# State-space stage of a decoder: silu written with tanh, layernorm taken on tokens, x loaded first, residual added by TensorE

## The chip, the cores and the metric

One core of a Trainium2 chip runs the whole program. The metric is device time in microseconds (us), from the start to the end of one execution. The engines work side by side and meet through semaphores: TensorE (PE; its weight loads are shown as PEld), VectorE (DVE), ScalarE (ACT), GpSimd (POOL) and SyncE (SP), which here only issues transfers. ScalarE can issue transfers too.

## The reference, cut to what matters

Eight sequences of 256 tokens with 128 channels, in fp32, pass through three parts. The first is a state-space layer, which holds most of the change:

```python
Xn = (X - mu) * lax.rsqrt(var + 1e-05) * ln_g + ln_b
x  = silu(causal_depthwise_conv(Xn @ W_up1.T, K=4) + conv_b)      # 256 channels
pp = x @ W_ll.T + b_ll                   # 256 delta, 16 B, 16 C
delta = softplus(pp[..., :256]);  A = -exp(A_log)
A_bar = exp(delta * A)                   # 256 x 16 for each token
U = x * (A_bar - 1) / (delta * A) * delta * B
H_t = A_bar_t * H_{t-1} + U_t;    y_t = sum_n C_t[n] * H_t[:, n]
out = X + (y * silu(Xn @ W_up2.T)) @ W_down.T + b_down
```

Its caller adds X once more and takes a layernorm, so that the kernel computes 2X plus the projection. The second part is cross-attention, 16 heads of 64 channels, against a context of the same shape; the queries' input and the context each have a layernorm ahead of their projections. The third part is six layers of windowed attention and feed-forward, which the change does not touch.

## The kernel before, in words

The work is cut into four pairs of sequences (NPAIR), each 512 tokens wide (TP). Tiles hold channels on the 128 partitions and the tokens of a pair along the free axis, so that x and the context, which lie in memory by tokens, are transposed by TensorE after loading (t_ps, lines 319 and 161). A layernorm (layernorm_steps, lines 104 to 148) therefore sums over partitions: TensorE multiplies by a matrix of 1/128 for the mean (ln_mu, L108) and for the variance of the centred squares (ln_var, L120), and the root of the variance is Ln followed by Exp on ScalarE (inv_root, reported at L92).

For one pair, pre(p) makes everything that the scan needs. It loads and transposes x, normalises it into xn, and runs the convolution as 2 halves x 4 taps of matmuls on shifted views of xn (conv, L329), with the tap weights multiplied into the projection's ahead of time (w_tap, L290). Silu gives xm (L340). From xm TensorE forms B and C (bc_ps, L345), which ScalarE writes to DRAM through its own queue (L353), and delta (d_ps, L358), of which softplus is made as max(d, 0) (z, L367) plus ln(1 + exp(-|d|)) (ez, L365 and L92). The sum is dt (L371). The gate is a second silu (L392).

scan(p) runs 16 states n by 2 halves h. For each: rows n of B and of C come back from DRAM, broadcast over all partitions (rows, L455, SP's queue, 4 buffers); VectorE forms wz from xm, rows and 1/A (L460); GpSimd takes the difference of neighbours in time (dw, L465); ScalarE takes the exp of dt times A (ab, into two PSUM buffers, reported at L92); VectorE runs the recurrence, one instruction for each sequence (m, L444); GpSimd multiplies by C (mc, L446, 6 buffers); TensorE adds mc into the sum y by a multiplication with the identity (L424). From n = 2 on, wz reads a copy of xm in PSUM (xm_ps, L432). post(p) multiplies y by the gate (yg, L403), projects it (dn_ps, L408), adds the bias (L411) and 2x (r, L412) and takes the layernorm.

While pair p is scanned, steps of post(p-1) and of pre(p+1) are taken between the states; during the last two scans they are steps of project(0), which prepares cross-attention for the first pair (layernorms of context and latents, q, k and v). project(1) to project(3) run in the cross-attention loop, whose rounds consist of scores (s_ps, L993), values (o_ps, L1012) and sums (L1018) on TensorE. Each engine runs its own instructions in a fixed order, settled when the program is built. ScalarE's functions come from tables that have to be loaded: silu has a table of its own, while exp and ln are in one that load_table (L96) brings back. behind_exps and issue_after place an instruction behind the exps that are already in the order:

```python
            for h in range(2):
                m = sp.tile([P, TP], FP, tag=f"xm{h}", name="xm")
                with behind_exps():
                    A.activation(m, acc[h], AF.Silu, bias=col("conv_b", h))
                xm.append(m)
            load_table()
```

## Time and profile before

| what | value |
|---|---|
| time, median of 3 runs | 2323.32 us (2321.04 to 2324.24) |
| the profiled execution | 2323.17 us |
| its span in the profile | 2321.2 us |
| mean granted TensorE clock | 0.974 |
| busy share: PE, DVE, ACT, POOL | 93%, 77%, 64%, 71% |
| instructions: PE, DVE, ACT, POOL | 20240, 2486, 2483, 1437 |
| GpSimd's product with C (L446) | 128 instructions of 1277 ns on average |
| transfers of rows (L455) | 128 of 256 KB, 3.9 us from issue to landing |
| transfers of x | 4 of 256 KB, 5.4 us from issue to landing |

The profile page cuts the span into 40 slices of 58 us and gives the busy share of each engine there in tenths. In a line of the timeline the first number is the start in us, the second the length, then come engine, line of the program, operation, output and inputs with their shapes; "x3" means three instructions in a row, and the brackets at the end hold the idle time of the engine ahead of the instruction and what ended it. A line of the waits gives engine, tile and line, what was waited for, and then the total in us, the number of waits and the longest.

### The profile page before, as it was taken

How to read it: one execution, taken by the hardware profiler on the slowest of the kernel's cores; microseconds unless marked ns; L12 is line 12 of the kernel's file. 1: busy time of each engine (PE TensorE's matmuls, PEld its weight loads, DVE VectorE, ACT ScalarE, POOL GpSimd, SP SyncE). 2: the span in 40 equal slices, each digit the busy share in tenths (PEclk: the TensorE clock that was granted, in tenths of full speed). 3: DMA queues.
4: the chain of work that ended last, by engine and by line, in shares of the span. 5: the costliest groups of instructions: out<-in, count | busy, mean ns of one | idle time of the engine just before them, and what ended most of it. 6: DMA issues, size and time to landing. Idle time of an engine off the chain costs nothing.

```text
span 2321.2 us, 52828 instructions
## 1 busy us (share of the span) xinstructions
PE 2166.6 (93%) x20240; PEld 1347.3 (58%) x20240; DVE 1784.3 (77%) x2486; ACT 1483.5 (64%) x2483; POOL 1645.1 (71%) x1437
## 2 busy tenths in 40 slices
PE   7876888999998999999999999999999999999986
PEld 3232333444445666666666666666666766666664
DVE  4788886454457888888888888888888888888873
ACT  4434454455556766777777677677766776777664
POOL 3888886232368887777787777777777777777760
PEclk9887899999999999999999999999999999999999
DMA  4343331000203334343343334333343434333331
GB/s 128 96 114 93 98 98 41 1 6 1 80 18 60 65 63 88 65 74 61 71 80 69 71 63 80 71 71 67 62 85 71 73 60 78 62 61 62 57 66 32
DMA packets 438517, 154.38 MB, mean 67 GB/s; under 512 B 401918, under 2 KB 418172, under 8 KB 438140
## 3 DMA queue, kind: packets, MB, share of 16 engines
q1 hardware_dynamic: 438076, 150.75, 32.8%
q8 instruction: 163, 2.67, 0.5%
q14 instruction: 86, 0.70, 0.1%
q10 hardware_dynamic: 192, 0.26, 0.0%
HBM read 55.20 MB, written 1.31 MB: 24 GB/s over the span
## 4 chain that ended last, share of the span: by engine, by line
PE 34%; DVE 21%; ACT 20%; POOL 10%; issue 6%; DMA 0%; SPq 0%; POOLq 0%; ACTq 0%; DVEq 0%
DVE rb L617 4%; DVE qk L616 4%; PE qk_ps L599 4%; ACT sq L622 4%; ACT kz L668 3%; POOL pw L717 3%; PE f_ps L836 3%; POOL qk L620 3%; ACT pw L92 3%; PE qkT_ps L655 3%; PE o_ps L750 2%; DVE ss L629 2%; PE y_ps L769 2%; PE v_ps L599 2%; PE pr L214 2%
## 5 line engine op out<-in xcount | busy, mean ns | idle before, releaser
L620 POOL TENSOR_TENSOR qk<-qk,rb 128x512 f32<-128x512 f32 x384 | 484.5, 1283 | 108.4 <-DVE rb L617 88.8
L648 POOL TENSOR_TENSOR qk<-qk,rn 128x1024 f32<-128x1024 f32 x192 | 366.3, 1908 | 133.7 <-ACT rn L92 108.0
L599 PE MATMUL qk_ps<-wqkv,xs 128*128 128x512 f32 x768 | 364.9, 598 | 2.0 <-ACT sq L622 2.0
L622 ACT ACTIVATE sq<-qk_ps 128x1024 f32<-128x1024 f32 x192 | 196.8, 1025 | 179.0 <-DVE rb L617 169.2
L616 DVE TENSOR_TENSOR qk<-qk_ps,tab 128x1024 f32<-128x1024 f32 x192 | 233.3, 1215 | 79.7 <-PE qk_ps L599 78.8
L717 POOL TENSOR_TENSOR pw<-pw,mx 128x512 f32<-128x512 f32 x192 | 200.3, 1043 | 92.1 <-DVE mx L716 87.2
L629 DVE TENSOR_REDUCE ss<-sq 128x16 f32<-128x1024 f32 x192 | 232.5, 1211 | 40.3 <-ACT sq L622 37.5
L617 DVE TENSOR_TENSOR rb<-qk_ps,tab 128x1024 f32<-128x1024 f32 x192 | 233.2, 1214 | 0.0
L655 PE MATMUL qkT_ps<-ident,qk 128*128 128x128 f32 x1536 | 209.1, 279 | 15.1 <-ACT v L642 9.9
L92 ACT ACTIVATE pw<-pw 128x512 f32<-128x512 f32 x192 | 120.5, 628 | 155.0 <-POOL pw L717 154.7
L668 ACT COPY kz<-qkT_ps 64x1024 f32<-64x1024 f32 x192 | 193.1, 1006 | 34.8 <-PE qkT_ps L655 33.2
L750 PE MATMUL o_ps<-vz,pT 128*32 128x128 f32 x6144 | 207.5, 276 | 8.2 <-ACT pT L742 8.2
L731 POOL TENSOR_TENSOR pw<-pw,mx 128x512 f32<-128x512 f32 x192 | 200.3, 1044 | 19.5 <-DVE mx L730 17.9
L769 PEld LDWEIGHTS y_ps<-oT,wo 128*128 128x128 f32 x1536 | 186.3, 192 | 44.6 <-issue 36.8
L729 DVE TENSOR_REDUCE mx<-pw 128x8 f32<-128x512 f32 x192 | 130.5, 680 | 105.5 <-ACT pw L92 104.9
L1002 POOL TENSOR_TENSOR ws<-w 128x512 f32<-128x512 f32 x64 | 81.4, 1273 | 181.4 <-ACT w L92 171.5
L750 PEld LDWEIGHTS o_ps<-vz,pT 128*32 128x32 f32 x6144 | 156.0, 110 | 91.7 <-ACT rn L92 36.4
L703 PE MATMUL s_ps<-kz,qT 128*32 128x128 f32 x6144 | 203.0, 273 | 0.0
L599 PE MATMUL v_ps<-wqkv,xs 128*128 128x512 f32 x384 | 185.5, 606 | 16.6 <-ACT kz L668 16.5
L655 PEld LDWEIGHTS qkT_ps<-ident,qk 128*128 128x128 f32 x1536 | 164.9, 141 | 55.2 <-issue 43.6
L446 POOL TENSOR_TENSOR mc<-m,rows 128x512 f32<-128x512 f32 x128 | 163.3, 1277 | 40.8 <-issue 12.8
L599 PEld LDWEIGHTS qk_ps<-wqkv,xs 128*128 128x128 f32 x768 | 131.6, 191 | 96.5 <-issue 92.2
(180 smaller groups left out, 4237.5 us busy)
## 6 DMA issues: line engine op xcount, KB each, us to landing
vz<-v SPq DMA_DIRECT2D x1152, 64.0 KB, 2.1
rows<-bc_dram SPq DMA_DIRECT2D x128, 256.0 KB, 3.9
vz<-v SPq DMA_DIRECT2D x576, 32.0 KB, 2.0
wqkv<-in_L_ffn_Wqkv SPq DMA_DIRECT2D x18, 512.0 KB, 4.2
wo<-in_L_ffn_Wo SPq DMA_DIRECT2D x48, 64.0 KB, 2.0
w<-in_L_ffn_W SPq DMA_DIRECT2D x6, 341.0 KB, 3.3
t_in<-in_x SPq DMA_DIRECT2D x4, 256.0 KB, 5.4
wkv<-in_L_xattn_Wkv SPq DMA_DIRECT2D x1, 1024.0 KB
```

The costliest lines, as they stand in the source:

```text
L599: T.matmul(pr[:, i * 512 : (i + 1) * 512], lhsT=got[n]["xs"][:, tb * P : (tb + 1) * P], rhs=thirds[seq[n][0], c][:, i * 512 : (i + 1) * 51 ...
L616: V.tensor_tensor(t, p3, cs, ALU.mult)
L617: V.tensor_tensor(rb, p3, sn, ALU.mult)
L620: G.tensor_tensor(t[:, :, o], t[:, :, o], rb[:, :, f], ALU.add)
L622: A.activation(sq, p3, AF.Square)
L629: V.tensor_reduce(got[n]["ss"][:, 2 * c + tb, :], got[n]["sq"], AX.X, ALU.add)
L648: G.tensor_tensor(t, t, r, ALU.mult)
L655: T.transpose(t_ps[:, hb * P : (hb + 1) * P], t[:, 2 * hb : 2 * hb + 2, :].rearrange("p h d -> p (h d)"), ident,)
L668: A.copy(fixed3["kzs"][0][r, :, e, W + tb * P : W + (tb + 1) * P], t3[r])
L717: G.tensor_tensor(pw, pw, mx[:, 0].unsqueeze(3).to_broadcast(shape), ALU.subtract)
L750: T.matmul(o_ps[i * W : (i + 1) * W, j * P : (j + 1) * P], lhsT=pT[:, j, i * W : (i + 1) * W], rhs=vz[:, j, i].rearrange("p e d -> p (e d) ...
L769: T.matmul(y_ps[:, :P], lhsT=wts[d][0][:, hb, :], rhs=got[n]["oT", wh][:, hb, :], start=(hb == 0), stop=(hb == NHB - 1),)
```

## The change

Silu is computed as half its argument times (1 + tanh of half its argument). The halves are folded into the weights (w_tap, w_up2, half_b); tanh is taken from the table set that also holds exp, then 1 is added on ScalarE (for xm) or inside the product (for the gate), and VectorE multiplies. The number of table loads stays. The load that brings ln back stands behind the write of B and C. x of each pair and the context of each pair are normalised while tokens are on the partitions: bn_stats and bn_aggr on VectorE give mean and variance, and subtraction and scaling are four instructions (on ScalarE for x of pairs 1 to 3, on VectorE otherwise); only the result is transposed, and scale and shift are applied on the way out of PSUM. x itself is transposed as well, for the residual. The first load is that of x; identity and columns come over ScalarE's queue. The tap weights are formed after the first steps of pre(0), and the last steps of pre(0), the gate among them, are taken during scan 0. For pair 0 the rows of B of states 0 and 1 are broadcast by TensorE out of bc. The maximum z moves to ScalarE for pairs 1 to 3. 2x is added by a third matmul into the projection.

```diff
@@ -68,10 +68,12 @@
     def ps_o(name):
         return banks[-1].tile([P, 512], FP, tag="o", name=name)
 
+    t_in0 = keep.tile([P, 4, D], FP, name="t_in0")
+    nc.sync.dma_start(out=t_in0, in_=a["x"][0:2].rearrange("b (c q) d -> q (b c) d", q=P))
     ident = keep.tile([P, P], FP, name="ident")
-    nc.sync.dma_start(out=ident, in_=a["c_ident"])
+    nc.scalar.dma_start(out=ident, in_=a["c_ident"])
     cols = keep.tile([P, NCOL], FP, name="cols")
-    nc.sync.dma_start(out=cols, in_=a["cols"])
+    nc.scalar.dma_start(out=cols, in_=a["cols"])
     mean_w = keep.tile([P, P], FP, name="mean_w")
     G.memset(mean_w, 1.0 / D)
     eps_t = keep.tile([P, 1], FP, name="eps_t")
@@ -91,10 +93,8 @@
         with tc.issue_after(table[-1].ins) if table else ExitStack():
             return f(*args, **kw)
 
-    def load_table():
-        table.append(
-            tc.keep_in_program_order(A.preload_act_table_set("natural_log_exp_and_others"))
-        )
+    def load_table(name="natural_log_exp_and_others"):
+        table.append(tc.keep_in_program_order(A.preload_act_table_set(name)))
 
     def inv_root(dst, src, bias=0.0):
 
@@ -151,15 +151,33 @@
         for _ in layernorm_steps(*args):
             pass
 
-    def load_transposed(src, p, dst, pool):
-        t_in = pool.tile([P, 4, D], FP, name="t_in")
-        nc.sync.dma_start(
-            out=t_in, in_=src[2 * p : 2 * p + 2].rearrange("b (c q) d -> q (b c) d", q=P)
-        )
+    def turned_tokens(t):
         tp = ps_s("t_ps")
         for j in range(4):
-            T.transpose(tp[:, j * P : (j + 1) * P], t_in[:, j, :], ident)
-        A.copy(dst, tp)
+            T.transpose(tp[:, j * P : (j + 1) * P], t[:, j, :], ident)
+        return tp
+
+    def layernorm_tokens(t, on_act=False):
+
+
+        st = lnp.tile([P, 4, 6], FP, name="bn_st")
+        mv = lnp.tile([P, 4, 2], FP, name="bn_mv")
+        for j in range(4):
+            V.bn_stats(st[:, j, :], t[:, j, :])
+            V.bn_aggr(mv[:, j, :], st[:, j, :])
+        rs = lnp.tile([P, 4], FP, name="ln_rs")
+        inv_root(rs, mv[:, :, 1], eps_t)
+        if on_act:
+            V.scalar_tensor_tensor(mv[:, :, 0], mv[:, :, 0], -1.0, rs, ALU.mult, ALU.mult)
+        for j in range(4):
+            if on_act:
+                A.activation(
+                    t[:, j, :], t[:, j, :], AF.Identity, bias=mv[:, j, 0:1], scale=rs[:, j : j + 1]
+                )
+            else:
+                V.tensor_scalar(
+                    t[:, j, :], t[:, j, :], mv[:, j, 0:1], rs[:, j : j + 1], ALU.subtract, ALU.mult
+                )
 
     def one_by_one(*gens):
         for g in gens:
@@ -189,11 +207,16 @@
 
         wq, wkv = w2["wq"], w2["wkv"]
         sp = pools2[0]
-        ct = sp.tile([P, TP], FP, name="ct")
-        load_transposed(a["ctx_1024"], p, ct, sp)
+        t_in = sp.tile([P, 4, D], FP, name="t_in")
+        nc.sync.dma_start(
+            out=t_in,
+            in_=a["ctx_1024"][2 * p : 2 * p + 2].rearrange("b (c q) d -> q (b c) d", q=P),
+        )
+        yield
+        layernorm_tokens(t_in)
         yield
         cn = sp.tile([P, TP], FP, name="cn")
-        yield from layernorm_steps(ct, cn, col("ctx_w"), col("ctx_b"), fine=not p)
+        A.activation(cn, turned_tokens(t_in), AF.Identity, bias=col("ctx_b"), scale=col("ctx_w"))
         yield
         la = sp.tile([P, TP], FP, name="la")
         yield from layernorm_steps(x1[p], la, col("lat_w"), col("lat_b"), fine=not p)
@@ -252,7 +275,6 @@
             )
             return t_in
 
-        t_in = load_x(0)
         w_up1 = wp.tile([P, DI], FP, name="w_up1")
         nc.sync.dma_start(out=w_up1, in_=a["w_up1T"])
 
@@ -279,18 +301,28 @@
 
 
         w_tap = wp.tile([P, 2, KC, P], FP, name="w_tap")
-        for h in range(2):
-            r_ps = ps_s("tap_ps")
-            for k in range(KC):
-                T.matmul(
-                    r_ps[:, k * P : (k + 1) * P],
-                    lhsT=col("conv_w", h * KC + k).to_broadcast([P, P]), rhs=ident,
-                    start=True, stop=True,
-                )
-            V.tensor_tensor(
-                w_tap[:, h], r_ps.rearrange("p (k c) -> p k c", k=KC),
-                w_up1[:, h * P : (h + 1) * P].unsqueeze(1).to_broadcast([P, KC, P]), ALU.mult,
-            )
+
+        def taps():
+            for h in range(2):
+                r_ps = ps_s("tap_ps")
+                for k in range(KC):
+                    T.matmul(
+                        r_ps[:, k * P : (k + 1) * P],
+                        lhsT=col("conv_w", h * KC + k).to_broadcast([P, P]), rhs=ident,
+                        start=True, stop=True,
+                    )
+                V.scalar_tensor_tensor(
+                    w_tap[:, h], r_ps.rearrange("p (k c) -> p k c", k=KC), 0.5,
+                    w_up1[:, h * P : (h + 1) * P].unsqueeze(1).to_broadcast([P, KC, P]),
+                    ALU.mult, ALU.mult,
+                )
+
+
+        half_b = wp.tile([P, 2], FP, name="half_b")
+        V.tensor_scalar(half_b, cols[:, _OFF["conv_b"] : _OFF["conv_b"] + 2], 0.5, None, ALU.mult)
+        V.tensor_scalar(w_up2, w_up2, 0.5, None, ALU.mult)
+        twice = wp.tile([P, P], FP, name="twice")
+        V.tensor_scalar(twice, ident, 2.0, None, ALU.mult)
 
         xns = [wp.tile([P, 2, KC - 1 + S], FP, name=f"xn{i}") for i in range(2)]
         for t in xns:
@@ -314,13 +346,15 @@
             x = new_x(p)
             t_in = t_in or load_x(p)
             yield
-            tp = ps_s("t_ps")
-            for j in range(4):
-                T.transpose(tp[:, j * P : (j + 1) * P], t_in[:, j, :], ident)
+            tp = turned_tokens(t_in)
             yield
             A.copy(x, tp)
+            layernorm_tokens(t_in, on_act=p > 0)
+            yield
+            tp = turned_tokens(t_in)
+            yield
             xn = xns[p % 2][:, :, KC - 1 :]
-            yield from layernorm_steps(x, xn, col("ssm_g"), col("ssm_b"), two, p > 0, wide=not p)
+            A.activation(xn, two(tp), AF.Identity, bias=col("ssm_b"), scale=col("ssm_g"))
             xm, gate, dt, acc = [], [], [], []
             got.update(x=x, xm=xm, gate=gate, dt=dt)
             for h in range(2):
@@ -332,14 +366,16 @@
                     )
                 yield
 
-            for _ in range(3 if p else 1):
+            for _ in range(2 if p else 0):
                 yield
+            load_table("exp_and_others")
             for h in range(2):
                 m = sp.tile([P, TP], FP, tag=f"xm{h}", name="xm")
                 with behind_exps():
-                    A.activation(m, acc[h], AF.Silu, bias=col("conv_b", h))
+                    with_table(A.activation, m, acc[h], AF.Tanh, bias=half_b[:, h : h + 1])
+                A.activation(m, m, AF.Identity, bias=1.0)
+                V.scalar_tensor_tensor(m, acc[h], half_b[:, h : h + 1], m, ALU.add, ALU.mult)
                 xm.append(m)
-            load_table()
             bc_ps = ps_s("bc_ps")
             for k in range(2):
                 T.matmul(
@@ -352,6 +388,25 @@
             bc = dp.tile([2 * NS, TP], FP, name="bc_dram")
             nc.scalar.dma_start(out=bc, in_=bc_sb)
             got.update(bc=bc)
+
+            got.update(b_ps=[])
+            for n in range(0 if p else 2):
+                t = ps1.tile([P, TP], FP, tag="ab", name="b_ps")
+                T.matmul(
+                    t, lhsT=ident[: 2 * NS, n : n + 1].to_broadcast([2 * NS, P]), rhs=bc_sb,
+                    start=True, stop=True,
+                )
+                got["b_ps"].append(t)
+
+            c_ps = ps_s("c_ps")
+            T.matmul(
+                c_ps[:NS], lhsT=ident[: 2 * NS, NS : 2 * NS], rhs=bc_sb, start=True, stop=True
+            )
+            cb = sp.tile([NS, TP], FP, name="cb", bufs=1)
+            got.update(cb=cb)
+            if p:
+                V.scalar_tensor_tensor(cb, c_ps[:NS], -1.0, bc_sb[:NS], ALU.mult, ALU.mult)
+            load_table()
             for h in range(2):
                 d_ps = ps_s("d_ps")
                 for k in range(2):
@@ -364,20 +419,17 @@
                 e = sp.tile([P, TP], FP, name="ez")
                 A.activation(e, d_ps, AF.Abs, bias=col("b_dt", h))
                 z = sp.tile([P, TP], FP, name="z", bufs=1)
-                V.tensor_scalar(z, d_ps, col("b_dt", h), 0.0, ALU.add, ALU.max)
+                if p:
+                    A.activation(z, d_ps, AF.Relu, bias=col("b_dt", h))
+                else:
+                    V.tensor_scalar(z, d_ps, col("b_dt", h), 0.0, ALU.add, ALU.max)
                 with_table(A.activation, e, e, AF.Exp, scale=-1.0)
-                soft = with_table(A.activation, e, e, AF.Ln, bias=1.0)
+                with_table(A.activation, e, e, AF.Ln, bias=1.0)
                 t = sp.tile([P, TP], FP, tag=f"dt{h}", name="dt")
                 (G if p else V).tensor_tensor(t, z, e, ALU.add)
                 dt.append(t)
-
-            c_ps = ps_s("c_ps")
-            T.matmul(
-                c_ps[:NS], lhsT=ident[: 2 * NS, NS : 2 * NS], rhs=bc_sb, start=True, stop=True
-            )
-            cb = sp.tile([NS, TP], FP, name="cb", bufs=1)
-            V.scalar_tensor_tensor(cb, c_ps[:NS], -1.0, bc_sb[:NS], ALU.mult, ALU.mult)
-            got.update(cb=cb)
+            if not p:
+                V.scalar_tensor_tensor(cb, c_ps[:NS], -1.0, bc_sb[:NS], ALU.mult, ALU.mult)
             yield
             g_ps = []
             for h in range(2):
@@ -386,10 +438,12 @@
                     g_ps[h], lhsT=w_up2[:, h * P : (h + 1) * P], rhs=xn, start=True, stop=True
                 )
             yield
+            load_table("exp_and_others")
             for h in range(2):
                 g = sp.tile([P, TP], FP, tag=f"gate{h}", name="gate")
-                with tc.issue_after(soft.ins), behind_exps():
-                    A.activation(g, g_ps[h], AF.Silu)
+                with behind_exps():
+                    with_table(A.activation, g, g_ps[h], AF.Tanh)
+                V.scalar_tensor_tensor(g, g, 1.0, g_ps[h], ALU.add, ALU.mult)
                 gate.append(g)
             load_table()
 
@@ -405,15 +459,15 @@
             yield
             d_ps = ps_s("dn_ps")
             for h in range(2):
-                T.matmul(d_ps, lhsT=w_dn[:, h, :], rhs=yg[h], start=(h == 0), stop=(h == 1))
+                T.matmul(d_ps, lhsT=w_dn[:, h, :], rhs=yg[h], start=(h == 0), stop=False)
+            T.matmul(d_ps, lhsT=twice, rhs=x, start=False, stop=True)
             yield
             r = pool.tile([P, TP], FP, tag=tags[2], name="r", bufs=1)
             A.activation(r, d_ps, AF.Identity, bias=col("ssm_bd"))
-            V.scalar_tensor_tensor(r, x, 2.0, r, ALU.mult, ALU.add)
             x1[p] = new_x(p)
             yield from layernorm_steps(r, x1[p], fine=True, wide=p == NPAIR - 1)
 
-        def scan(p, x, xm, gate, dt, bc, cb, steps, spare):
+        def scan(p, x, xm, gate, dt, bc, b_ps, cb, steps, spare):
 
 
             y = [ps_o("y0"), ps_o("y1")]
@@ -450,7 +504,8 @@
             for n in range(NS):
 
                 rows = sp.tile([P, 2, TP], FP, name="rows", bufs=4)
-                for i in range(2):
+                early = n < len(b_ps)
+                for i in range(1 if early else 0, 2):
                     r = i * NS + n
                     nc.sync.dma_start(out=rows[:, i, :], in_=bc[r : r + 1, :].to_broadcast([P, TP]))
                 for h in range(2):
@@ -458,7 +513,8 @@
                     w = wzs.pop(0)
                     wzs.append(w)
                     V.scalar_tensor_tensor(
-                        w[:, :, 1:], two((xm if n < 2 else xp1)[h]), ia[:, c : c + 1], two(rows[:, 0, :]),
+                        w[:, :, 1:], two((xm if n < 2 else xp1)[h]), ia[:, c : c + 1],
+                        two(b_ps[n] if early else rows[:, 0, :]),
                         ALU.mult, ALU.mult,
                     )
                     dw = sp.tile([P, TP], FP, name="dw", bufs=3)
@@ -500,12 +556,13 @@
                     yield
 
         nxt = {}
-        ahead = pre(0, nxt, t_in)
-        next(ahead)
+        last = pre(0, nxt, t_in0)
+        for _ in range(3):
+            next(last)
+        taps()
         decay()
-        for _ in ahead:
-            pass
-        last = iter(())
+        for _ in range(7):
+            next(last)
         for p in range(NPAIR):
             cur, nxt = nxt, {}
             if p == 1:
```

## The prediction

> **What bounds the kernel now.** I read the page first (busy shares and slices), then a table of windows over the first 540 us, where every edited line lies, then GpSimd's waits there, then the order of time on ScalarE, GpSimd, TensorE and VectorE around the stalls.
>
> ```profile
> span 2321.2 us, 52828 instructions
> PE   7876888999998999999999999999999999999986
> POOL 3888886232368887777787777777777777777760
> ```
>
> One slice is 58 us. GpSimd is the fullest engine only in slices 2 to 6, the state-space stage (it ends at 382). After that TensorE is.
>
> ```profile
> 37.00:105.00 68.00, 54.36 (x112) 19.87 (x112) 52.71 (x83) 33.05 (x48) 56.91 (x50) 0.85 0.41 107
> 105.00:175.00 70.00, 53.96 (x125) 21.96 (x124) 61.20 (x93) 25.90 (x41) 63.21 (x56) 0.81 0.44 114
> 400.00:470.00 70.00, 69.45 (x346) 33.20 (x344) 31.19 (x40) 36.06 (x57) 16.33 (x14) 1.00 0.02 4
> ```
>
> Columns: window, length, busy us (instructions) of PE, PEld, DVE, ACT, POOL, granted clock, DMA share, GB/s. In the scans GpSimd works 57 of 68 and 63 of 70 us, VectorE 53 and 61, ScalarE only 33 and 26. In cross-attention TensorE works 69.5 of 70 and ScalarE and VectorE half. So a scan loses time where GpSimd stalls, cross-attention where TensorE gets work.
>
> ```profile
> POOL dw L465 <- DVE wz L460: 38.1, 4, 35.9
> POOL mc L446 <- issue: 12.8, 4, 5.8
> POOL mc L446 <- PE bc_ps L345: 11.8, 2, 7.1
> POOL mc L446 <- PE pr L214: 6.1, 1, 6.1
> ```
>
> 35.9 us is the prologue. Most of the rest are two waits in each scan, both set by exps (ab) that ScalarE could not issue while it waited on the next pair's silu, as pair 1 shows:
>
> ```profile
> 58.59 1.28 ACT L340 ACT_TABLE_LOAD   x1
> 65.39 0.69 ACT L340 ACTIVATE xm<-conv,cols 128x512 f32<-128x512 f32 x1 [5.53 <-PE conv L329]
> 68.83 0.69 ACT L340 ACTIVATE xm<-conv,cols 128x512 f32<-128x512 f32 x1 [2.75 <-PE conv L329]
> 69.53 1.28 ACT L96 ACT_TABLE_LOAD   x1
> 70.83 1.30 ACT L92 ACTIVATE ab<-dt,aa 128x512 f32<-128x512 f32 x2
> ...
> 43.10 1.26 POOL L446 TENSOR_TENSOR mc<-m,rows 128x512 f32<-128x512 f32 x1 [1.67 <-DVE m L444]
> 72.95 1.26 POOL L446 TENSOR_TENSOR mc<-m,rows 128x512 f32<-128x512 f32 x1 [7.06 <-PE bc_ps L345]
> ```
>
> No exp ends from 58.56 to 70.83 (12.3 us), and GpSimd stalls 7.43 (0.37 at 61.3, 7.06 here). By this count the silu stalls of pairs 1 to 3 are 7.43, 5.92 and 7.61. The gate's silu leaves gaps of 7.2, 10.9 and 14.9 us and stalls of 1.85, 4.73 and 6.08, together 12.7. Gap less stall is 4.8 to 8.8: ScalarE may be away about 4.8 us before GpSimd runs dry.
>
> **The change, part by part.** The sum is against the profiled execution, 2323.17 us (0.15 below the median), 2 us of it outside the span.
>
> *Prologue.* Before, x is third on SP; its transposes run at 7.87, and mean, centring, squares, variance, two wide activations, a table load and two scalings follow, so that conv starts at 18.18. After, x is first and two tables move to ACT's queue. The page has 5.4 us from issue to landing for such a load: x by about 5 (3.8 to 5.9). Statistics are eight short DVE instructions; no row shows bn_stats, so between 0.18 (128x32) and 0.42 (128x256) each: to 7.1. Ln and Exp of 128x4 (0.26, 0.20), four normalisations behind the first w_tap product in VectorE's queue (tap_ps moved behind x's transposes): 8.9 to 9.9. Transposes 1.12 cold, xn 0.69: conv at about 12.8, 5.4 earlier. Its 16 passes last 9.52 as before. Behind them, before: silu, load, bc, bc's write, rows from DRAM, and wz at 36.23. After: tanh, +1, product, bc, and two rows broadcast by TensorE, wz at about 27. The first scan then needs dt: d_ps now stands behind c_ps and b_ps; Abs at about 30.8, exp at 34.05 (before 39.10). The first mc comes at about 37.05 instead of 43.10: -6.05. Pair 0's gate (3.8 us of ScalarE and two DVE products) lands in scan 0: +1.3, between 0 and 4. **-4.7** (-7 to -2).
>
> *Silu of pairs 1 to 3.* Behind conv's last pass stood silu 0.69 and a load 1.28, then the exp: 2.0. Now stand tanh 0.69 (not in the trace; activations of this size take 0.57 to 0.69), +1 0.59, the DVE product 0.75, the second half of bc_ps 0.95, bc 0.66, the load 1.28: 4.9. **3.0 longer** each. bc_ps gets queued on TensorE behind up to six y matmuls in pairs 2 and 3. Against it, exp shares tanh's table, and the order has two exps between the load and the first tanh, worth 0 to 4.4 (two steps of 2.2, 128 of which make up the scans). I take 1.3 off per pair, the lower half, because m and its buffers also limit those two: 3 x 1.7 = **+5** (-4 to +12).
>
> *Gate of pairs 1 to 3.* The order after is exp, exp, load, tanh, tanh, load, exp, exp; copies and softplus steps no longer crowd ahead of it. ScalarE is away 1.28+0.69+0.69+1.28 = 3.9 us, under the 4.8 of cover; with g_ps late by 1.5, as in pair 3, 5.4. Of 12.7 us about 1.7 stays: **-11** (-12 to -6).
>
> *Other work in the scans.* Per pair VectorE loses centring 0.69, xn 0.75+0.47, z 2x0.73 and the residual 0.69 (4.1) and gains eight statistics at 0.3 and 4x0.75 (5.4, or 4.5 with the shortest): nothing is freed there. ScalarE gains some 3.7 us a pair (two +1, four normalisations, two Relu, xn, less a square and a wide one), beside 33 of 68 busy; its cover gone, that would cost 3.7 a pair. The residual by TensorE removes an instruction that GpSimd's traffic stretched:
>
> ```profile
> 232.71 4.13 DVE L412 SCALAR_TENSOR_TENSOR r<-x,r 128x512 f32<-128x512 f32 x1
> ```
>
> Such a product takes 0.73 to 0.75 elsewhere, and GpSimd stalls 1.86 and 1.73 behind it. **-1** (-4 to 0), since tensors in SBUF remain elsewhere. The Trainium skill ("SBUF — State Buffer", the shared port) says VectorE and GpSimd lock each other out over one port in such operations; the stretched row agrees.
>
> A rule against the change: "ScalarE: Activation LUTs" (operation-to-engine table) wants relu on VectorE, not ScalarE. Here z as Relu is 0.69 us of an engine half idle, against 0.73 of VectorE; by the rule the sum would lose what ScalarE's rows show, nothing. The same page (what ACT_TABLE_LOAD costs) adds a drain of about 1.38 us to each load; here the exp starts 1.30 after its load starts. By the page the gate gap would be an estimated 6.7 and half its gain gone.
>
> *Cross-attention.* The context's layernorm on tokens takes mean and variance off TensorE, the full engine:
>
> ```profile
> 398.11 1.14 PE L993 MATMUL s_ps<-qT,kT 64*128 64x256 f32 x8
> 399.18 1.08 PE L1012 MATMUL o_ps<-w,v 128*64 128x256 f32 x8
> 400.09 0.60 PE L1018 MATMUL o_ps<-ws,ones 128*64 128x256 f32 x4
> 400.62 1.13 PE L120 MATMUL ln_var<-ln_sq,mean_w 128*128 128x512 f32 x2
> 401.68 1.14 PE L993 MATMUL s_ps<-qT,kT 64*128 64x256 f32 x8
> ...
> 404.19 1.13 PE L993 MATMUL s_ps<-qT,kT 64*128 64x256 f32 x8
> ```
>
> A round with a variance takes 3.57 us (398.11 to 401.68), one without 2.51: 1.06 each, with no gap. Pairs 1 to 3 lose two each there: -6.4; the residual matmul of pair 3 adds 0.9. **-5.5** (-7 to -2, if the normalised tokens come late to transposes queued in order).
>
> Sum: -4.7+5-11-1-5.5 = -17.2, so 2306.0.
>
> **The rivals.** (a) *The gate stalls stay.* For it: the copies and softplus that crowded ScalarE must all still run, and tanh needs VectorE's product before yg. Against: the order spreads them. The -11 is gone: -6.2, 2317; with silu at +9 it is -2, 2321.
> (b) *Slower: the next exp hangs on VectorE and TensorE.* The load that lets exps resume now stands behind bc, hence behind two DVE products and bc_ps. VectorE is 61 of 70 busy, its queue holds wz that wait for rows, and the clock granted is 0.81. All other terms give -22.2, so it decides from 7.4 us a pair (silu stalls near 14, twice before). A wz waiting on rows 3.09 us in pair 2 and the 4.13 row on VectorE, both ahead of the product, plus 3 make 10.2 a pair: +8.4, 2331.6.
> (c) *x no earlier.* Three loads start at once and x lands as late as before: the -4.7 goes to 0, 2310.7.
> (d) *Cross-attention gains nothing,* the four normalisations on VectorE coming late to TensorE's queue: 2311.5. Against: 31 of 70 busy.
>
> **How the numbers follow.** A run of this kernel can tell about 0.2%, 4.6 us, from no change: faster is below 2318.7, slower above 2328. Forecast 0.60, (a) 0.18, half of it inside 0.2%, (b) 0.10, most of it slower, (c) 0.07 and (d) 0.05, both faster. Faster 0.60+0.09+0.12, less 0.02 for mixtures = 0.79; same 0.12; slower 0.09. The forecast's own range from the bounds, not all met at once, is 2296 to 2316; to (a)'s end it reaches 2321.
>
> **What would show it.** Right: the first mc near 37; the gate of pairs 1 to 3 with load to load under 4.5 us and no GpSimd stall over 2; silu stalls of 8 to 9; rounds in cross-attention of 2.5 us with the mean and variance of ct gone. Wrong: GpSimd waiting over 12 us behind bc_ps, or TensorE waiting on t_in in cross-attention. From 540 us on nothing changes, so the end of pair 3's projection should already show the whole difference.

## The result and the profile after

The changed kernel takes 2311.45 us (median of 5 runs, 2309.95 to 2316.58) against 2324.24 us for the kernel before, measured beside it (5 runs, 2321.04 to 2325.79). The ratio is 0.9951, with a 95% interval from 0.9936 to 0.9965: faster by 0.5%, a gain of 12.8 us where 17.2 were predicted. The profiled execution took 2310.31 us, its span is 2308.5 us and its mean granted clock 0.976.

From the page of the changed kernel:

```profile
PE   7776888999999999999999999999999999999986
POOL 3889795232478878777787777787877777777760
```

TensorE still fills the span after the scans. GpSimd's seventh digit falls from 6 to 5: its scans end 8.6 us earlier in that slice.

A window of the changed kernel over the first scan, with the columns of before:

```profile
37.00:105.00 68.00, 50.76 (x101) 18.10 (x102) 51.64 (x91) 38.25 (x59) 55.25 (x50) 0.87 0.36 90
```

ScalarE has 38 us of work in the first scan instead of 33 and is still the least busy of the three engines of the scan. TensorE stays full in cross-attention (69.18 of the 70 us from 390 on).

GpSimd's longest waits in the changed kernel over the scans (37 to 382 us): engine, tile and line, what it waited for, total us, number, longest.

```profile
POOL mc L500 <- PE d_ps L413: 18.7, 2, 11.0
POOL mc L500 <- DVE m L498: 10.9, 3, 9.4
POOL mc L500 <- PE ln_mu L108: 8.3, 1, 8.3
```

18.7 and 8.3 are the silu stalls of pairs 1 to 3: 11.01, 7.68 and 8.33 us, all larger than before. The waits at the gates are almost gone (0.22, 0.33, and 0.64 with 0.86). The 10.9 is mostly the prologue (9.4). The names on the right are what ended last by the record; ScalarE's timeline shows what held the exps, here for pair 1:

```profile
58.20 0.67 ACT L94 ACTIVATE ab<-dt,aa 128x512 f32<-128x512 f32 x1
...
63.87 0.69 ACT L94 ACTIVATE xm<-conv,half_b 128x512 f32<-128x512 f32 x1 [4.29 <-PE conv L363]
...
67.30 0.69 ACT L94 ACTIVATE xm<-conv,half_b 128x512 f32<-128x512 f32 x1 [2.08 <-PE conv L363]
...
71.44 0.68 ACT L386 ACTIVATE bc<-bc_ps,cols 32x512 f32<-32x512 f32 x1 [2.79 <-PE bc_ps L381]
...
72.50 1.28 ACT L97 ACT_TABLE_LOAD   x1 [0.39 <-ACT bc L386]
73.80 1.30 ACT L94 ACTIVATE ab<-dt,aa 128x512 f32<-128x512 f32 x2
```

No exp ends from 58.87 to 73.80, 14.9 us where it was 12.3. ScalarE idles 4.29, 2.08 and 2.79 us in it with a table loaded that holds exp.

The gate of pair 1 in the changed kernel, on ScalarE:

```profile
87.80 1.28 ACT L97 ACT_TABLE_LOAD   x1
89.09 1.25 ACT L94 ACTIVATE gate<-g_ps 128x512 f32<-128x512 f32 x2
90.36 1.28 ACT L97 ACT_TABLE_LOAD   x1
91.66 0.69 ACT L94 ACTIVATE ab<-dt,aa 128x512 f32<-128x512 f32 x1
```

From the last exp's end (87.78) to the next exp's start is 3.9 us; before it was 7.2. In pairs 2 and 3 it is 5.5 and 3.7, where it was 10.9 and 14.9.

One round of cross-attention with the context's transposes, on TensorE in the changed kernel:

```profile
388.55 1.14 PE L1050 MATMUL s_ps<-qT,kT 64*128 64x256 f32 x8
...
391.06 0.66 PE L157 MATMUL t_ps<-ident,t_in 128*128 128x128 f32 x4
391.64 1.14 PE L1050 MATMUL s_ps<-qT,kT 64*128 64x256 f32 x8
```

Where the transposes fall, the round takes 3.09 us; the mean and variance of ct are gone.

The difference can be added up along the time. "First" and "last" are the starts of the first and last product with C on GpSimd; a stall is GpSimd's idle time, a silu stall with the small one just ahead of it (1.21 and 1.79 before, 1.43 after), as the prediction counted it; "layers" is the start of the first matmul of the third part.

| | first | silu stalls, pairs 1, 2, 3 | gate stalls, sum | last | layers |
|---|---|---|---|---|---|
| before | 43.10 | 7.43, 5.92, 7.61 | 12.7 | 379.20 | 624.2 |
| changed | 37.25 | 11.01, 7.68, 9.76 | 2.1 | 370.62 | 611.4 |
| difference | -5.9 | +7.5 | -10.6 | -8.6 | -12.8 |

Between first and last, besides silu and gate, stand +1.3 (a stall of 1.27 after pair 0's gate), -1.2 (the stalls near 240 us, 3.59 to 2.44), -1.6 (other stalls) and +1.9 (GpSimd's own instructions longer). From 370.62 to 611.4 cross-attention gives 4.2 more. From there on nothing changes.

### The profile page after: what moved, and what is told of

Its sections match the earlier page's. It is cut to its first block, busy times and chain, and to the rows that moved or that the text cites. A ratio compares the mean times of both kernels' runs of the same rounds, so it can differ in the third digit from the quotient of the medians.

```text
span 2308.5 us, 52803 instructions
## 1 busy us (share of the span) xinstructions
PE 2149.5 (93%) x20194; PEld 1337.3 (58%) x20194; DVE 1784.3 (77%) x2558; ACT 1489.8 (65%) x2505; POOL 1645.3 (71%) x1437
## 4 chain that ended last, share of the span: by engine, by line
PE 31%; ACT 21%; DVE 20%; POOL 9%; issue 6%; DMA 1%; SPq 0%; POOLq 0%; ACTq 0%; DVEq 0%
DVE rb L674 5%; DVE qk L673 5%; PE qk_ps L656 4%; ACT sq L679 4%; ACT kz L725 3%; POOL pw L774 3%; PE f_ps L893 3%; POOL qk L677 3%; ACT pw L94 3%; DVE ss L686 2%; PE qkT_ps L712 2%; PE o_ps L807 2%; PE y_ps L826 2%; PE s_ps L1050 2%; DVE mx L786 2%
## 5 line engine op out<-in xcount | busy, mean ns | idle before, releaser
L500 POOL TENSOR_TENSOR mc<-m,rows 128x512 f32<-128x512 f32 x128 | 164.5, 1288 | 40.5 <-PE d_ps L413 18.7
L826 PE MATMUL y_ps<-oT,wo 128*128 128x128 f32 x1536 | 187.2, 275 | 0.1
```

Source lines behind the costliest of these rows:

```text
L826: T.matmul(y_ps[:, :P], lhsT=wts[d][0][:, hb, :], rhs=got[n]["oT", wh][:, hb, :], start=(hb == 0), stop=(hb == NHB - 1),)
```

## The experiments

Except where said, each starts from the changed kernel. Ratios are to the kernel before.

**The context's layernorm by channels again.**

```diff
-        layernorm_tokens(t_in)
-        yield
-        cn = sp.tile([P, TP], FP, name="cn")
-        A.activation(cn, turned_tokens(t_in), AF.Identity, bias=col("ctx_b"), scale=col("ctx_w"))
+        ct = sp.tile([P, TP], FP, name="ct")
+        A.copy(ct, turned_tokens(t_in))
+        yield
+        cn = sp.tile([P, TP], FP, name="cn")
+        yield from layernorm_steps(ct, cn, col("ctx_w"), col("ctx_b"), fine=not p)
```

> Only the context's layernorm goes back to channels (transposed first, mean and variance by TensorE); all else is the changed kernel. Theory: the 4.5 us gained between 382 us and the end of cross-attention are the mean and variance taken off a full TensorE, so they go again: rounds with such a matmul take 3.57 instead of 2.51 us, 4.5 to 6.4 us more in all, about 2316.5 against 2311.45. Rival: the gain there comes from the earlier projection of pair 0 or other order; then the time stays within 1 us of 2311.5.

2317.77 us, ratio 0.9970 (0.9956 to 0.9985). From the first scores of cross-attention to the first matmul of the layers the kernel before takes 241.9 us (382.28 to 624.2), the changed one 237.4 (374.00 to 611.4), this one 242.3 (374.32 to 616.6). The gain there is the context's layernorm and nothing else. It also shows a cost of that edit that was not expected: the stall of 2.25 us near 245 us is gone here, though other stalls grew as much (pair 3's silu 10.6 us), and the scans as a whole were no shorter (334.3 us from the first to the last product with C, 333.4 in the changed kernel). In the changed kernel VectorE shows this just ahead of that stall:

```profile
239.21 3.56 DVE L178 TENSOR_SCALAR t_in<-t_in,bn_mv,ln_rs 128x128 f32<-128x128 f32 x2
```

Two normalisations of the context took 3.56 us beside GpSimd; the other two of the same pair took 0.59 together.

**The load behind xm, ahead of bc** (the gate's load tied behind softplus, so that it cannot pass it).

```diff
                 xm.append(m)
+            load_table()
             bc_ps = ps_s("bc_ps")
...
-            load_table()
             for h in range(2):
                 d_ps = ps_s("d_ps")
```

> The load that brings back the table of ln and exp stands right behind the second half of xm, ahead of bc, as in the kernel before; the gate's load is tied behind softplus. Theory A: the product on VectorE, bc_ps and bc, about 2.4 to 4.4 us a pair, leave the chain to the next exp, so GpSimd's silu stalls fall from 11.0, 7.7 and 8.3 us to about 8, 5 and 6, and the time to about 2303 to 2306. Theory B: the late load is also what spread softplus and the xm_ps copies among the exps; then the gate's stalls come back at 2 to 5 us a pair, and the time stays at 2309 to 2315.

2317.80 us, ratio 0.9975 (0.9965 to 0.9985): theory B, even beyond its range. The silu stalls are 10.77, 7.75 and 5.36 us, 4.6 less in sum; the gates stall 1.78, 4.78 and 5.96 us, 12.5 in sum, as before the change. (The first product with C came 3.1 us earlier in the profiled execution, at another clock; the last section comes to that. From there to the last one it took 339.8 us, 6.5 more.) The gate of pair 1 here:

```profile
86.19 1.28 ACT L97 ACT_TABLE_LOAD   x1
90.23 0.60 ACT L94 ACTIVATE gate<-g_ps 128x512 f32<-128x512 f32 x1 [2.75 <-PE g_ps L437]
...
93.00 1.30 ACT L94 ACTIVATE ab<-dt,aa 128x512 f32<-128x512 f32 x2
```

6.8 us from exp to exp, since the load is issued before g_ps is there. In ScalarE's order the gate's load stands behind the 20th, 58th and 90th exp (counted over all scans) here and in the changed kernel alike; what moved is what stands around it. In the changed kernel the second half of softplus has three exps between it and that load, in each pair; here it has two, none and none. The copies of xm in pairs 2 and 3 stand two exps or more behind the gate there, and here between its load and its first activation. So the gate's gain hangs on where the load after silu stands: with the load behind bc, softplus comes earlier among the exps and the copies later, and the gate stands free of both.

**The gate by silu again.**

```diff
-            load_table("exp_and_others")
...
-                    with_table(A.activation, g, g_ps[h], AF.Tanh)
-                V.scalar_tensor_tensor(g, g, 1.0, g_ps[h], ALU.add, ALU.mult)
+                    with_table(A.activation, g, g_ps[h], AF.Silu, scale=2.0)
```

> The gate alone goes back to the silu function (argument doubled by the instruction's scale), in its new place and without its product on VectorE; xm keeps tanh. Theory: the gate's stalls (12.7 us before, 2.1 after) fell by the order, since both ways have two loads and two activations; they stay under 1 us a pair and the time at 2309 to 2312. Rival: tanh out of the exp table is what lets exps go on; then the stalls return at 2 to 4 us a pair, and the time is 2318 to 2322.

2322.75 us, ratio 1.0001 (0.9992 to 1.0010). The time is that of the rival: the whole gain is gone, though two loads and two activations stand where they stood. For pairs 1 and 2 the theory was nearly right all the same: their gates stall 0.87 and 1.06 us (0.22 and 0.33 with tanh, 1.85 and 4.73 before), from gaps of 5.4 and 5.6 us. The gates stall 7.9 us in sum (after 2.1), 5.0 of them at one place in pair 3, where ScalarE's order now puts two copies that wait for the projection of pair 0 ahead of the exps. And pair 1's silu, which was not edited, stalls 15.3 instead of 11.0 us. VectorE in this run:

```profile
70.66 0.75 DVE L513 SCALAR_TENSOR_TENSOR wz<-xm_ps,ia,rows 128x512 f32<-128x512 f32 x1 [3.48 <-DMA rows<-bc_dram]
71.32 1.40 DVE L377 SCALAR_TENSOR_TENSOR xm<-conv,half_b,xm 128x512 f32<-128x512 f32 x2
```

The first product of xm had its inputs at 63.05 us and ran at 71.32, behind a wz that waited for its rows. TensorE's bc_ps waited 5.31 us for it. The same pair in the changed kernel:

```profile
67.97 0.75 DVE L515 SCALAR_TENSOR_TENSOR wz<-xm_ps,ia,rows 128x512 f32<-128x512 f32 x1 [1.01 <-DMA rows<-bc_dram]
...
68.72 1.38 DVE L377 SCALAR_TENSOR_TENSOR xm<-conv,half_b,xm 128x512 f32<-128x512 f32 x2
```

Its inputs were there at 65.22, and it ran at 68.72; bc_ps waited 0.52 us. That is rival (b) of the prediction at work, at a small price in the changed kernel and a larger one here.

**xm by silu again,** with the load right behind it and the gate tied behind softplus.

```diff
-            load_table("exp_and_others")
...
-                    with_table(A.activation, m, acc[h], AF.Tanh, bias=half_b[:, h : h + 1])
-                A.activation(m, m, AF.Identity, bias=1.0)
-                V.scalar_tensor_tensor(m, acc[h], half_b[:, h : h + 1], m, ALU.add, ALU.mult)
+                    A.activation(m, acc[h], AF.Silu, bias=col("conv_b", h), scale=2.0)
                 xm.append(m)
+            load_table()
```

> xm goes back to the silu function (argument doubled by the scale) with the load of ln and exp right behind it; the gate keeps tanh, tied behind softplus. Theory: the silu stalls go back to 6 to 8 us a pair (21 us before, 27 after), but the order crowds softplus and the copies ahead of the gate as it did with the early load, and the gate's stalls come back at 2 to 6 us: 2313 to 2320. Rival: the tanh of xm has only cost; without it the time is 2305.

2316.32 us, ratio 0.9968 (0.9956 to 0.9980), as the theory had it. The silu stalls are 11.34, 6.66 and 4.71, 22.7 in sum; the gates cost 16.8 in sum (5.2, 5.3 and 6.3 with the small ones beside them). The first product with C came at 31.11 us, 6.1 earlier than in the changed kernel, in part because TensorE had its clock there (0.95 over 22 to 32 us, 0.50 in the changed kernel). So the tanh of xm costs some 6 us in its own stalls and more in the prologue; it is not what pays. The load that comes with it, behind bc, is.

**No rows from TensorE for pair 0.**

```diff
-            for n in range(0 if p else 2):
+            for n in range(0):
```

> Rows of B of states 0 and 1 come from DRAM again instead of four matmuls at 0.95 us (3.78 us) that stand ahead of c_ps and d_ps while pair 0 waits for its first exp. Theory: d_ps moves 3.8 us up (27.3 to 23.5), the first exp from 34.6 to about 31 and the first product with C from 37.25 to about 33.5: about 2307.7. Rival: the rows, which came 5.8 us behind the write of bc in the kernel before, get VectorE's wz late (28 instead of 23.9), and dw and the first m with it; then the first product with C comes at 36 to 38 and the time stays at 2311.

2311.17 us, ratio 0.9958 (0.9944 to 0.9972). d_ps started at 23.74 as expected, but the first wz ran at 30.21, so the first product with C came at 35.99 instead of 37.25; pair 1's silu then stalled 13.09 us. The rival is right.

**Identity and columns first, x third.**

```diff
-    t_in0 = keep.tile([P, 4, D], FP, name="t_in0")
-    nc.sync.dma_start(out=t_in0, in_=a["x"][0:2].rearrange("b (c q) d -> q (b c) d", q=P))
...
-    nc.scalar.dma_start(out=ident, in_=a["c_ident"])
+    nc.sync.dma_start(out=ident, in_=a["c_ident"])
...
+    t_in0 = keep.tile([P, 4, D], FP, name="t_in0")
+    nc.sync.dma_start(out=t_in0, in_=a["x"][0:2].rearrange("b (c q) d -> q (b c) d", q=P))
```

> Identity and columns are loaded first again over SP's queue, and x third, all else as in the changed kernel. Theory: x was issued 0.93 us later in the kernel before, so conv starts about 1 us later (11.6 against 10.65) and the end is 1 us later, 2312.5; most of the 7.5 us by which conv came earlier is layernorm on tokens and the tap weights moved behind x's transposes. Rival: x shares the engines with the loads beside it and lands as late first as third: no change.

2315.62 us, ratio 0.9962 (0.9948 to 0.9976). Conv starts at 11.55 instead of 10.65, and every later mark is 0.9 to 1.2 us later (first 38.21, last 371.55, layers 612.6). That is the expected microsecond; the median's further 3 us are not in the trace, and the intervals overlap.

**The residual on VectorE again.**

```diff
-            T.matmul(d_ps, lhsT=twice, rhs=x, start=False, stop=True)
...
+            V.scalar_tensor_tensor(r, x, 2.0, r, ALU.mult, ALU.add)
```

> The residual goes back from a third matmul to a product on VectorE with both inputs in SBUF. Theory: GpSimd's stalls of 2.25 and 1.43 us near 245 to 251 us stay in the changed kernel without that product, so they are not its work; it takes 0.75 us on VectorE, up to 4 us where GpSimd's traffic meets it, and cross-attention saves the 0.95 us matmul of pair 3: 2310 to 2313. Rival: the 4.13 us of before come back for every pair and hold up wz: about 2315.

2311.16 us, ratio 0.9943 (0.9930 to 0.9957). No difference from the changed kernel (0.9951); the stalls near 245 us are there (1.74 at 243.4), and the layers start at 611.4 in both. The residual by TensorE is worth nothing that can be measured.

**Exps among the tanhs:** a yield behind each half of xm.

```diff
                 xm.append(m)
+                if p:
+                    yield
```

> Only a yield more behind each half of xm for pairs 1 to 3, so that steps of the running scan come between; on ScalarE six exps (pair 1) or exps on both sides of each tanh (pairs 2 and 3) then stand between the two loads, where there were two in front of both. Theory: the silu stall is ScalarE's order, the exps could go on under the table they share with tanh while conv and bc_ps run; the stalls of 11.0, 7.7 and 8.3 us fall to 2 to 4 each, and the time to 2294 to 2300. Rival: the stall is the chain of xm, bc_ps and the rows itself, or a later preparation of the next pair gives it back at the gate or at the start of the next scan; then the time stays above 2306.

2312.58 us, ratio 0.9958 (0.9944 to 0.9972): no better, and in the profiled execution the scans were longer (336.7 us from the first to the last product with C, 333.4 in the changed kernel), behind a prologue that was 3.3 us shorter, most of it by the clock. Pair 1's silu stall fell from 11.01 to 6.32, those of pairs 2 and 3 did not (8.3 and 9.9 with the small ones ahead), and the gates took 7.3 in place of 2.1, 4.3 of it in pair 3. The second product of pair 1 had its inputs at 65.5 us and ran at 70.33, behind four wz.

**Every wz behind the newest product of xm.**

```diff
                 prods.append(V.scalar_tensor_tensor(m, acc[h], half_b[:, h : h + 1], m, ALU.add, ALU.mult))
...
+                    with tc.issue_after(prods[-1].ins):
                         V.scalar_tensor_tensor(
                             w[:, :, 1:], two((xm if n < 2 else xp1)[h]), ia[:, c : c + 1],
```

> In the changed kernel the products that make xm stand in VectorE's order behind wz of later states, which wait for rows, whose buffers are freed by the stalled products with C. Here every wz is tied behind the newest product of xm; nothing else is edited. Theory: that queue is part of the silu stall: the product of pair 1's first half waited 3.5 us, those of pairs 2 and 3 stand behind up to four wz; the three stalls (27.0 us) fall by 3 to 8 us, to about 2305. Rival: the chain through conv's end, bc_ps and the load sets the stall whatever VectorE does, and the wz that now come after the products are late for dw: the stalls stay within 2 us of 27 and the time at 2311.

2310.02 us, ratio 0.9935 (0.9920 to 0.9950). The three stalls with the small ones beside them are 10.3, 8.8 and 7.7, 26.8 in sum: the rival. In pair 1 VectorE was then held by something else: statistics of pair 2's x stood ahead of the product and waited 4.77 us for their load, as the next run but one shows too. In pair 2 the products did run earlier, and it changed nothing: bc_ps started 5.24 us behind the start of the y matmuls ahead of it, as in the changed kernel.

**Pair 0's delta first.**

```diff
-            got.update(b_ps=[])
-            for n in range(0 if p else 2):
...
                 dt.append(t)
+                if not (p or h):
+                    for n in range(2):
+                        t = ps1.tile([P, TP], FP, tag="ab", name="b_ps")
...
+            if not p:
+                c_ps = ps_s("c_ps")
```

> For pair 0 the first half of d_ps goes ahead of the rows that TensorE broadcasts, and c_ps behind the second half. Theory: b_ps and c_ps (3.0 us at the full clock, 5.7 at half) leave the path to the first exp, while wz still gets its rows by 27 to 29: the first product with C at about 33 instead of 37.25 where the clock is granted at half from 22 us on, and the time about 3 to 4 us less, 2308. Rival: wz and dw become the last to arrive, and the first product with C stays at 36 to 37.

2307.47 us, ratio 0.9926 (0.9910 to 0.9943). The first product with C came at 30.87 us, 6.4 earlier, more than expected, and the last at 366.47, 4.2 earlier. More, because TensorE kept its clock. Windows of the changed kernel, and then of this one:

```profile
22.00:32.00 10.00, 10.00 (x12) 3.18 (x13) 3.63 (x6) 2.11 (x3) 3.03 (x3) 0.50 0.53 164
```

```profile
22.00:32.00 10.00, 7.63 (x17) 2.15 (x15) 7.80 (x12) 6.79 (x10) 4.61 (x4) 1.00 0.51 164
```

In the changed kernel TensorE is busy for all 10 us at half the clock, b_ps takes 3.78 us for four matmuls and d_ps runs to 33.3. Here d_ps follows bc_ps with no gap, the clock is 1.00 and b_ps takes 1.98.

**All three:** the yields, wz behind products, and delta first.

> The two edits above together with the yield behind each half of xm. Theory: with products no longer behind wz, the exps set free by the yields are not paid for in VectorE's queue; silu stalls near 4 us a pair, first product with C near 33, gate stalls up to 5 in pair 3: 2298 to 2304. Rival: what one link of the chain gives back, the next takes (the gate moves behind more states and meets the next scan's copies and the projection of pair 0): no better than the changed kernel, 2309 to 2313.

2309.65 us, ratio 0.9932 (0.9918 to 0.9947): the rival. First product with C at 30.69, but silu stalls of 8.1, 10.0 and 10.0 us. VectorE in pair 1:

```profile
59.62 0.49 DVE L166 BATCH_NORM_STATS2 bn_st<-t_in 128x6 f32<-128x128 f32 x2 [4.78 <-DMA t_in<-in_x]
...
60.76 0.72 DVE L378 SCALAR_TENSOR_TENSOR xm<-conv,half_b,xm 128x512 f32<-128x512 f32 x1
```

The statistics of a later pair's x had moved ahead of this pair's product, and waited 4.78 us for their load.

**The queue cleared:** all three, and the statistics tied behind the newest recurrence step.

```diff
+            with tc.issue_after(behind.ins) if behind else ExitStack():
                 V.bn_stats(st[:, j, :], t[:, j, :])
                 V.bn_aggr(mv[:, j, :], st[:, j, :])
```

> The three edits of the run before, and the token statistics of a later pair's x are tied behind the newest recurrence step (m) on VectorE: in the run before, VectorE stood 4.8 us before the first product of pair 1, waiting for the load of pair 2's x for these statistics. Theory: the silu stall is head-of-line waiting on VectorE (wz on rows, statistics on x) plus the chain; with both out of the way and exps among the tanhs, the stalls of pairs 1 and 2, 8.1 and 10.0 us in the run before, fall to 3 to 5 each, that of pair 3 stays near 7 to 10 and its gate near 5: 2298 to 2303. Rival: the chain from conv's end to the load is long enough by itself: the stalls stay at 6 to 9 and the time at 2306 to 2310, no better than with delta first alone.

2304.93 us (5 runs, 2303.89 to 2307.73), ratio 0.9917 (0.9903 to 0.9930): faster than both kernels, its interval lies below that of the changed one; against delta first alone (0.9910 to 0.9943) the difference is not clear of noise. The silu stalls are 5.4, 8.0 and 7.3 us, 20.7 in sum against 28.1 in the run before; the first product with C at 31.18, the last at 363.90. GpSimd's waits for wz fell in all three pairs (6.03 to 3.40, 4.56 to 2.75, 2.74 to 1.19). Pair 1 comes close to what the theory asked, pair 2 does not, and the gate of pair 3 still costs 5.1. The time lies between the two expectations. What held pair 2 was TensorE:

```profile
161.93 2.07 PE L487 MATMUL y<-mc,ident 128*128 128x512 f32 x2 [1.10 <-POOL mc L509]
163.94 2.60 PE L386 MATMUL bc_ps<-xm,w_ll 128*32 128x512 f32 x4
```

The second product of xm had ended at 154.28; bc_ps started 9.7 us later, behind y matmuls that waited for GpSimd's products.

## Why the prediction was right, point by point

The direction and the range held, and so did the sizes of prologue and gate; the silu term was too small, the contention term had the wrong sign, the cross-attention term was too large, and the sum was 4.4 us too large.

*Prologue.* Predicted 6.05 earlier and 1.3 lost in scan 0; measured 5.85 and 1.27. The total is right by luck: two errors cancel. Conv started at 10.65, not 12.8, since x's transposes could start at 4.11, and its 16 passes took 7.11 us, not 9.52. So the first wz ran at 23.91, not 27; this lead went again from 22 to 32 us, where TensorE ran at a clock of 0.50. Of the 7.5 us by which conv started earlier than before, loading x first is worth 0.9 (the run with x third); layernorm on tokens and the later tap weights, which are left for the rest, were not split by a run.

*Silu.* Predicted +5 with a bound of +12; measured +7.5. The chain behind conv was right in kind and undersized in every pair. In pair 1 it took 6.5 us from conv's end (67.26) to the exp (73.80), where 4.9 was reckoned. The first product ran 3.5 us late in VectorE's queue, and TensorE waited for it:

```profile
69.50 1.90 PE L381 MATMUL bc_ps<-xm,w_ll 128*32 128x512 f32 x4 [0.52 <-DVE xm L377]
```

So bc_ps ran its four passes (1.90) behind that product instead of its second half alone (0.95) behind the second one, and bc's write held the load for 0.39 more. The prediction named this queue in rival (b) but put it outside its own term.

In pairs 2 and 3 the chain took 9.4 and 9.7 us, and there it was not VectorE that held it. This is pair 2, whose second product ended at 166.40:

```profile
161.90 5.31 PE L478 MATMUL y<-mc,ident 128*128 128x512 f32 x12
167.14 1.90 PE L381 MATMUL bc_ps<-xm,w_ll 128*32 128x512 f32 x4
```

TensorE took up bc_ps without a gap behind twelve y matmuls, and so it did in pair 3 (246.97 to 252.21). The prediction saw them ("queued on TensorE behind up to six y matmuls", of two passes each) and gave them no price; this is the step of its sum that was mis-sized. Why the stalls of these pairs grew by only 1.8 and 2.1 us, though their chains grew by 7, was not followed.

The runs on VectorE's queue fit this. Where the queue grew (the gate by silu), pair 1 stalled 15.3 us. Tying wz behind the products did not shorten the chain of pair 2, and with the statistics tied as well bc_ps there still stood behind y matmuls. That clearing TensorE's queue ahead of bc_ps would pay is not shown: no run did it.

*Gate.* Predicted -11 from a gap of 3.9 us; measured -10.6 from gaps of 3.9, 5.5 and 3.7. The prediction gave two causes: tanh and its two loads fit under the cover, and copies and softplus no longer crowd ahead of the gate. In pairs 1 and 2 the second is the larger one. The run with the early load has the same tanh but the crowd is back, and it stalls as before; the run with the gate by silu has the new order without tanh, and stalls 0.87 and 1.06 us there. What the prediction missed is where the order comes from: the load behind bc, which it counted as a cost of the silu term alone. Pair 3 is open: with silu in the new place its gate stalls 6.0 us, with tanh 1.5, and two copies that wait for the projection stand ahead of the exps in the one and behind the first exp in the other. What in the fixing of the order moved them was not shown, nor why an edit of the gate makes pair 1's silu wait longer for its rows.

*Contention.* Predicted -1, with the residual's stretched product gone. The stalls near 240 us fell by 1.2, but GpSimd's instructions took 1.9 more in sum, and the residual by itself is worth nothing: the stretched instruction beside GpSimd is now one of the context's normalisations, 3.56 us for two. The prediction has no term for those. Stalls elsewhere, for which it has none either, fell by 1.6.

*Cross-attention.* Predicted -5.5; measured -4.2 between the last product with C and the layers. The mean and variance removed are as reckoned, shown by the run with the old context. Waits of TensorE that were not there before take 0.7 of the difference: 0.4 more for ln_sq and 0.3 for w. Another 0.3 passes before the first scores (3.4 us behind the last product with C, 3.1 before).

*The page rules.* "ScalarE: Activation LUTs" (what ACT_TABLE_LOAD costs) adds a drain to each load; the gate's gap with two loads is 3.9 us in pair 1 and the tanh starts 1.29 us after its load's start, so no drain shows here. Its rule against relu on ScalarE was not isolated by a run.

## What to carry to other kernels

On an engine that runs in order, a cheap instruction put into a chain is priced by what stands ahead of it, not by its own length. Look on each engine of the chain: here a product on VectorE stood behind instructions that waited for a transfer in pair 1, and four matmuls on TensorE stood behind twelve others in pairs 2 and 3. Moving one load or one function re-sorts the instructions around it: here the largest gain came from the place of a table load whose own effect was a cost, so the parts of such a change don't add up one by one. And where TensorE's clock is in question, closing a gap in its work can be worth more than the order alone: delta first gained 6.4 us at the first product with C where 4 were expected.

## What the runs showed of the hardware

The granted clock of TensorE fell to 0.50 at 21.7 us in the changed kernel and stayed there for 10.2 us in which TensorE was busy but for the first 0.1, after idle gaps of 1.25 and 0.77 us from 18.7 us on. The same gaps led to means of 0.50, 0.51, 0.53, 0.55, 0.66 and 0.83 over 22 to 32 us in different kernels with the same matmuls, and with it to anything from 3.78 to 1.98 us for b_ps. So the first product with C came at 37.25 us in the changed kernel and at 33.90 in the run with exps among the tanhs, whose edit touches pairs 1 to 3 only: 3 us for no reason in the code, as much as several edits here are worth. Without the second gap the mean was 1.00 in all three runs that had none of it (delta first, and the two built on it).

How long the half clock lasted can be added up from windows of 1 us (a mean of 0.62 is 0.76 us at half):

| run | granted clock, us by us | at half |
|---|---|---|
| changed kernel | 0.86 from 21 us, nine times 0.50, 0.52, then 1.00 | 10.2 us |
| gate by silu | 0.92 from 23 us, six times 0.50, 0.67, then 1.00 | 6.8 us |
| exps among the tanhs | 0.62 from 24 us, 0.50, 0.50, 0.67, then 1.00 | 3.4 us |

TensorE was busy in all three stretches, and their lengths are as three, two and one. The Trainium skill ("TensorE: Matmul & The Clock Gate", the HAM clock gate) says that the window that decides is free-running, which fits the scatter, and that some 3.4 us of sustained work bring the full clock back. The last row agrees; in the other two it took two and three times that, and why is open.

bn_stats of 128x128 took 0.26 us and bn_aggr 0.16, tanh of 128x512 out of PSUM 0.69, the same as other activations.
